# A four-block cross-attention network with routed experts: roots, routing pieces and weight loads of block 4

## The chip, the cores and the metric

The program runs on one core of a Trainium2 chip. Its time is the device time of one execution in microseconds (us); several executions are made and the median counts. All data are float32. The names of the engines are those of the profile: PE is the matrix engine, PEld its weight loads, DVE the vector engine, ACT the scalar engine, POOL GpSimd, SP the engine that issues most DMA transfers.

## What is computed

There are 16 sequences of 128 tokens with 256 features. Four blocks follow one another, each a cross-attention to a context and a feed-forward part, both behind a gate:

```python
x = x + tanh(g_xattn[i]) * xattn_i(layernorm(x), ctx)
x = x + tanh(g_ffn[i])   * ffn_i(layernorm(x))
```

Blocks 2 to 4 have routed experts in their feed-forward part (8 with 2 chosen, 16 with 4 chosen, 64 with 8 chosen). The change is mostly in block 4. Its attention has 16 heads of 16 features. Queries and keys are layer-normalised head by head, and the keys are of two kinds, each with a softmax of its own whose results are added:

```python
kv_dca = (y_dca @ Wkv_dca + bkv_dca)          # last 16 context tokens
k_dca, v_dca = ln(kv_dca[..., 0], ...), kv_dca[..., 1]
q = ln(x @ Wq + bq)                           # per head, eps 1e-6
k, v = ln(y_main @ Wk + bk), y_main @ Wv + bv # first 112 context tokens
ctx = attn(q, k, v) + attn(q, k_dca, v_dca)
return ctx @ Wo + bo
```

and its feed-forward part has 64 experts of width 96 and room for 128 tokens each:

```python
probs = softmax(x @ router_weight.T)
topw, topi = top_k(probs, 8);  topw = topw / topw.sum()
pos = position of the token among those of the same expert, in order
xe[topi, pos] = x                              # dropped where pos >= 128
h = silu(xe @ gate) * (xe @ up);  ye = h @ down
y = sum over the 8 chosen of topw * ye[topi, pos]
```

## The kernel before

**What stays where.** All of x lies in SBUF (`x_sb`, 128 tokens by 16 sequences by 256 features) for the whole program. Weights and context come by DMA; the rows for the experts go through two DRAM tensors per block, `xs_f` (rows sent to the experts) and `y_f` (the experts' results, by token and choice).

**Routing** (class `Routed`, lines 100 to 290) of a block's feed-forward part runs inside the attention before it. When the attention has added its result to x for the second sequence of a pair, `done` queues that pair's pieces, and each `tick` of the attention's loop runs the ones that are due: `stats`, `rows` (normalised rows into `hx`), `turn` (transposes), `logits`, `top` (the eight largest), `first` (the chosen experts as a mask and the weights), `places` (prefix sums as matmuls), `targets` (rows `hrow` in `xs_f`), then the sends. In block 4 there are four send pieces per pair, each with four indirect DMAs that POOL issues (L240), so 8 for each of the 16 sequences, 128 in all. A send is kept in order after the latest per-head normalisation on POOL (`mark`). What is left over runs in `finish`, at the start of the feed-forward part.

**Results of block 3's experts** are added to x late: `settle` fetches a sequence's four results of 128 x 256 (`fetch`, a DMA of 512 KB by SP into one of two buffers) and adds them with four dependent DVE instructions (`add`, L287). In block 4's attention the settles and the layer normalisation of x are placed by `norm_steps(sp, -3, 4)` in groups of four sequences: group 0 ahead of the loop, and for the groups 1 to 3 the settles eight to five iterations before they are needed, but never before iteration 0.

**Block 4's attention** (`xattn3`, from line 1250) is a loop over `b` in 0 to 17. In iteration `b` it works on several sequences at once. PE, DVE and ACT run in the order in which the loop is written (`manual_schedule`, L1441); POOL and SP are ordered by the scheduler. In the order of the loop:

- `normalise_qk(b+2)`: sums of squares per head (L1322), then the inverse root on DVE (`inverse_root`, L392: an integer guess and three Newton steps, twelve small instructions with the scaling), then two multiplications on POOL (L1327).
- `scores(b)` (32 small matmuls into four PSUM banks), and `maxima(b, ...)` of bank 0 (L1376), which are written beside the queries so that the next product subtracts them.
- `add_up(b-1)` (sums of exponentials, and their reciprocals `rd`, L1413) and `values(b-1)`, then the maxima of banks 1 to 3.
- `project(b-2)`: the output product (L1436), a further matmul that adds the bias (L1437), and the addition to x (L415).
- `quotients(b-1)`: `rd` spread over the heads (L1425), copied by ACT, multiplied into `aT` (L1430).
- `tick(b-2)`.
- `with_maxima(b)` (queries turned again), `project_qk(b+3)`, `exponentials(b)` (32 matmuls, then four ACT exponentials, L1389), `project_v(b)`, `squares(b+3)` and `turn_qk(b+2)`.
- the normalisation steps of this iteration, and a second `tick`.

The layer normalisation of x takes its inverse root from POOL (`power`, L390). PSUM is shared out as four banks `sc`, two `tr`, one `av` and one `pj`.

**The experts of block 4** (`ffn3`). A loop over steps `n`, with SP and PE in written order: `load(n)` (gate and up weights `wgu`, 192 KB in one of five buffers, and the expert's 128 rows `xe`, 140 KB in one of four), `load_down(n-1)` (`wdn`, 96 KB, five buffers), `up(n-3)`, `turn(n-2)`, `down(n-4)`. `turn` transposes `xe` (L795), and `destination` (L262 to L269) works out on DVE the row in `y_f` to which each result goes (`drow`, six buffers). `down` ends with an indirect DMA by POOL (L273). Every `xe` has to wait for all sends of the routing.

**Store.** For each sequence the eight results are fetched (1024 KB, four buffers), added by eight DVE instructions, and x is written out.

Of the kernel before, what the change touches and what calls it, by code (L numbers as in the profile page):

```python
# [91 lines left out]
class Routed:  # L92
# [24 lines left out]
    def done(self, b):  # L117

        if b % 2 == 1:
            for i, f in enumerate(self.pieces(b // 2)):  # L120
                self.due.setdefault(self.now + 1 + i, []).append(f)

    def tick(self):
        self.now += 1
        for f in self.due.pop(self.now, ()):
            f()

    def finish(self):
        self.net.mark = None
        for n in sorted(self.due):  # L130
            for f in self.due[n]:
                f()
        self.due = {}

    def pieces(self, p):
        net, nc, sp, E, K = self.net, self.net.nc, self.sp, self.E, self.K
        b0 = 2 * p
# [6 lines left out]
        def stats():  # L144
            h["stats"] = net.ln_stats(sp, b0, 2)

        def rows():
            x = tile("x", [P, 2, self.W], bufs=4)
            net.ln_rows(sp, b0, h["stats"], 2, to=x)

        def turn():
            net.ln_turn(b0, [h["x"][:, j, 0:D] for j in range(2)])

        def logits():
            lg = net.psum("tr", [P, 2, E])
            for j in range(2):
# [4 lines left out]
            mx = tile("mx", [P, 2])  # L161
            nc.vector.tensor_reduce(mx, lg, AX.X, ALU.max)
            sh = tile("sh", [P, 2, E])
            nc.vector.tensor_tensor(sh, lg, mx.unsqueeze(2).to_broadcast([P, 2, E]), ALU.subtract)
# [3 lines left out]
        def top():  # L168
            top, idx, x = tile("top", [P, 2, 8]), tile("idx", [P, 2, 8], U32), h["x"]
            for j in range(2):  # L170
                nc.vector.max(top[:, j, :], h["sh"][:, j, :])
                nc.vector.max_index(idx[:, j, :], top[:, j, :], h["sh"][:, j, :])
            nc.vector.tensor_copy(x[:, :, D : D + K], idx[:, :, 0:K])
            nc.vector.tensor_copy(x[:, :, D + K : D + 2 * K], self.ids[:, b0 : b0 + 2, :])
            w = tile("w", [P, 2, K])
            nc.scalar.activation(w, top[:, :, 0:K], AF.Exp)
            if self.over_all:
                nc.scalar.activation(tile("ex", [P, 2, E]), h["sh"], AF.Exp)

        def chosen():  # L180

            m, x = tile("m", [P, 2, E]), h["x"]
            if K == 8:
                for j in range(2):
                    nc.vector.match_replace(m[:, j, :], h["top"][:, j, :], h["sh"][:, j, :], 1.0)
                nc.vector.tensor_scalar(m, m, 0.5, None, ALU.is_gt)
            else:
                iota = net.cst[:, C_IOTA : C_IOTA + E].unsqueeze(1).to_broadcast([P, 2, E])
                for k in range(K):
                    dst = m if k == 0 else tile("m1", [P, 2, E])  # L190
                    nc.vector.tensor_tensor(dst, x[:, :, D + k : D + k + 1].to_broadcast([P, 2, E]), iota, ALU.is_equal)
                    if k:
                        nc.vector.tensor_tensor(m, m, dst, ALU.add)
            for j in range(2):
# [4 lines left out]
        def weights():  # L199
            den = tile("den", [P, 2])  # L200
            nc.vector.tensor_reduce(den, h["ex"] if self.over_all else h["w"], AX.X, ALU.add)
            nc.vector.reciprocal(den, den)
            nc.vector.tensor_scalar(den, den, self.gate, None, ALU.mult)
            nc.vector.tensor_tensor(
                h["x"][:, :, D + 2 * K :], h["w"], den.unsqueeze(2).to_broadcast([P, 2, K]), ALU.mult
            )

        def places():
            pos = net.psum("tr", [P, 2, E])
# [4 lines left out]
                pf, net.ones, self.before[:, b0 : b0 + 2, :].rearrange("p b e -> p (b e)"), start=False, stop=True  # L214
# [3 lines left out]
        def targets():  # L218
# [4 lines left out]
            enc = tile("enc", [P, 2, E])  # L223
            base = net.cst[:, self.base : self.base + 2 * E].rearrange("p (b e) -> p b e", b=2)
            nc.vector.tensor_tensor(enc, pos, base, ALU.add)
            nc.vector.tensor_tensor(enc, enc, m, ALU.mult)
            r8 = tile("r8", [P, 2, 8])
            for j in range(2):
                nc.vector.max(r8[:, j, :], enc[:, j, :])
            row = tile("row", [P, 2, K], U32, bufs=4)  # L230
            if self.spare:
                own = tile("own", [P, 2, K])
                nc.vector.tensor_scalar(own, self.ids[:, b0 : b0 + 2, :], float(-self.tiles * P), None, ALU.add)
# [15 lines left out]
        sends = [partial(send, j, range(k, k + many)) for j in range(2) for k in range(0, K, many)]  # L249

        def first():
            chosen()
            weights()
# [30 lines left out]
    def add(self, b, yg):  # L284
        x = self.net.x[:, b, :]
        for k in range(self.K):
            self.net.nc.vector.tensor_tensor(x, x, yg[:, k, :], ALU.add)  # L287


class Net:  # L290
    def __init__(self, tc, ctx, t, out):
# [17 lines left out]
        self.head = self.routed = None  # L309

# [81 lines left out]
    def inverse_root(self, v, n):  # L392
# [3 lines left out]
        half = self.sb(self.small, "half", [P, n], I32)  # L396
        nc.vector.tensor_scalar(half, v.bitcast(I32), 1, None, ALU.logical_shift_right)
        guess = self.sb(self.small, "guess", [P, n], I32)
        nc.vector.tensor_scalar(guess, half, -1.0, float(0x5F3759DF), ALU.mult, ALU.add)
        y = guess.bitcast(F32)  # L400
        for _ in range(3):
            t = self.sb(self.small, "nt", [P, n])
            nc.vector.tensor_tensor(t, y, y, ALU.mult)
# [1263 lines left out]
```

## Time and profile before

| what | us |
|---|---|
| runs | 2452.39, 3353.52, 2457.0 |
| median | 2457.0 |
| profiled execution | 2455.75 |
| its span | 2453.8 |
| mean granted clock of PE | 0.924 |

By the shares of the page PE is busy for 81% of the span, DVE for 60%, ACT for 36%, POOL for 33%. The stages follow one another with little overlap. Their borders, read from the timeline:

| stage | from, us | to, us |
|---|---|---|
| block 1 | 0 | 485 |
| block 2, attention and experts | 485 | 950 |
| block 3, attention | 950 | 1510 |
| block 3, experts | 1510 | 1822 |
| block 4, entry of the attention (weights, constants, first normalisations) | 1822 | 1860 |
| block 4, attention loop | 1860 | 2174 |
| block 4, only routed rows are sent | 2174 | 2232 |
| block 4, 64 experts | 2232 | 2385 |
| last additions and output | 2385 | 2454 |

A timeline line shows the start, the duration, engine, source line, operation, the tiles written and read with their shapes, how many instructions stand together, and in square brackets the engine's idle time before them with what ended it. In the waits, each line gives engine and waiting operation, what it waited for, then the total, the number of waits and the longest.

### The profile page before, as it was taken

To read this page: it belongs to the slowest core of one execution; us is meant where nothing else is said; L and a number is where in the kernel's file an instruction comes from. 1 tells how busy PE (TensorE), PEld (TensorE's weight loads), DVE (VectorE), ACT (ScalarE), POOL (GpSimd) and SP (SyncE) were. 2 spreads that over 40 slices of the span, in tenths; PEclk is the share of its full clock that TensorE was granted. 3 is DMA by queue.
4 is the path that set the end of the run, shared out by engine and by line. 5 is a ranking of instruction groups with operands and counts; after the bars stand their busy time and mean duration, and the time that the engine had idled before them with its cause. 6 is when DMAs were issued, how large, how long until landed. Compare 5 with 4: busy or idle time off the path is not lost. (4 is left out here: it accounts for less than half of the span.)

```text
span 2453.8 us, 38199 instructions
## 1 busy us (share of the span) xinstructions
PE 1998.5 (81%) x12988; PEld 1404.4 (57%) x12988; DVE 1483.7 (60%) x4176; ACT 879.1 (36%) x1868; POOL 806.2 (33%) x799
## 2 busy tenths in 40 slices
PE   8999998788887786999898997899965878744760
PEld 5776675356665553666565665566644766633550
DVE  4676765378986444666667665455556676432438
ACT  3433333266663123444443443122212434211320
POOL 1121111143544222334444444222230035564440
PEclk9999998899998899999999999999986899767995
DMA  5159951109201772000000001578752001226768
GB/s 178 69 134 270 303 154 35 52 2 343 94 19 55 230 245 76 18 1 25 21 21 21 16 17 67 182 245 250 247 194 69 19 27 67 74 93 194 243 220 291
DMA packets 198529, 299.32 MB, mean 122 GB/s; under 512 B 21514, under 2 KB 151025, under 8 KB 195905
## 3 DMA queue, kind: packets, MB, share of 16 engines
q1 hardware_dynamic: 175776, 238.90, 32.7%
q0 software_dynamic: 19488, 55.31, 6.1%
q10 hardware_dynamic: 3072, 2.68, 0.3%
q8 instruction: 105, 1.72, 0.3%
q14 instruction: 88, 0.71, 0.1%
HBM read 160.92 MB, written 135.90 MB: 121 GB/s over the span
## 5 line engine op out<-in xcount | busy, mean ns | idle before, releaser
L548 POOL TENSOR_TENSOR e<-e,r 128x512 f32<-128x512 f32 x128 | 132.7, 1037 | 565.7 <-DVE r L547 284.9
L273 POOL DMA_INDIRECT y_f<-ys,drow x182 | 174.5, 959 | 394.7 <-DVE ys L1076 212.0
L240 POOL DMA_INDIRECT xs_f<-hx,hrow x224 | 221.5, 989 | 105.9 <-issue 56.5
L536 ACT ACTIVATE e<-e 128x512 f32<-128x512 f32 x128 | 80.7, 630 | 476.2 <-DVE e L533 476.2
L1054 PE MATMUL mm<-wgu,xeT 128*128 128x352 f32 x472 | 166.9, 477 | 8.8 <-DVE xeT L1047 6.6
L1163 PE MATMUL qk<-wa,xnT 128*128 128x512 f32 x256 | 127.3, 620 | 24.0 <-DVE nq L1177 23.9
L543 DVE TENSOR_REDUCE sm<-e 128x4 f32<-128x512 f32 x128 | 87.8, 686 | 93.1 <-ACT e L536 93.1
L795 PE MATMUL tr<-cst,xe 128*128 128x128 f32 x364 | 72.3, 281 | 77.8 <-DMA xe<-xs_f 77.4
L1074 PE MATMUL o<-wdn,hT 88*128 88x256 f32 x472 | 122.0, 381 | 2.0 <-ACT hT L1067 2.0
L667 PE MATMUL y<-wb,aT 128*128 128x256 f32 x512 | 121.2, 380 | 1.0 <-DVE x_sb L415 1.0
L667 PEld LDWEIGHTS y<-wb,aT 128*128 128x128 f32 x512 | 97.3, 190 | 41.6 <-issue 18.2
L1216 PE MATMUL y<-wb,aT 128*128 128x256 f32 x512 | 121.0, 380 | 0.0
L633 PE MATMUL mm<-xnT,wm 128*128 128x512 f32 x256 | 120.1, 594 | 0.0
L795 PEld LDWEIGHTS tr<-cst,xe 128*128 128x128 f32 x364 | 46.3, 144 | 123.4 <-issue 85.3
L390 POOL TENSOR_TENSOR rr<-ss,nhalf 128x8 f32<-128x8 f32 x64 | 105.9, 1655 | 29.4 <-DVE ss L1171 29.3
L287 DVE TENSOR_TENSOR x_sb<-x_sb,yg 128x256 f32<-128x256 f32 x224 | 93.4, 423 | 32.0 <-DMA yg<-y_f 26.1
L1177 DVE TENSOR_TENSOR nq<-qk,rr 128x512 f32<-128x512 f32 x64 | 44.2, 691 | 113.1 <-POOL rr L390 113.1
L1067 ACT COPY hT<-tr 88x256 f32<-88x256 f32 x118 | 43.4, 368 | 181.5 <-PE tr L1065 181.3
L873 DVE TENSOR_REDUCE mx<-sc 128x4 f32<-128x512 f32 x128 | 84.6, 681 | 37.7 <-PE sc L866 37.7
L1054 PEld LDWEIGHTS mm<-wgu,xeT 128*128 128x128 f32 x472 | 81.7, 193 | 43.3 <-DVE xeT L1047 14.7
L521 PEld LDWEIGHTS tr<-cst,e 128*128 128x128 f32 x512 | 63.4, 141 | 69.9 <-issue 60.8
L1216 PEld LDWEIGHTS y<-wb,aT 128*128 128x128 f32 x512 | 92.7, 191 | 11.3 <-issue 1.2
(287 smaller groups left out, 4777.5 us busy)
## 6 DMA issues: line engine op xcount, KB each, us to landing
wgu<-in_L_W SPq DMA_DIRECT2D x118, 352.0 KB
xs_f<-zeros SPq DMA_DIRECT2D x32, 1072.0 KB
wdn<-in_L_W SPq DMA_DIRECT2D x118, 176.0 KB
xs_f<-zeros SPq DMA_DIRECT2D x16, 1048.0 KB
y_f<-zeros SPq DMA_DIRECT2D x16, 1024.0 KB
yg<-y_f SPq DMA_DIRECT2D x16, 1024.0 KB
wgu<-in_L_gu SPq DMA_DIRECT2D x64, 192.0 KB
xe<-xs_f SPq DMA_DIRECT2D x79, 134.0 KB
```

The costliest lines, as they stand in the source:

```text
L240: ins = nc.gpsimd.indirect_dma_start(out=self.rows, out_offset=bass.IndirectOffsetOnAxis(ap=h["row"][:, j, k : k + 1], axis=0), in_=h["x"] ...
L273: self.net.unordered("y_" + self.name, self.net.nc.gpsimd.indirect_dma_start(out=self.y, out_offset=bass.IndirectOffsetOnAxis(ap=row, axis ...
L287: self.net.nc.vector.tensor_tensor(x, x, yg[:, k, :], ALU.add)
L390: return self.nc.gpsimd.tensor_tensor(out, var, self.nhalf[:, :n], ALU.pow)
L548: nc.gpsimd.tensor_tensor(e, e, r.unsqueeze(2).to_broadcast([P, 4, S]), ALU.mult)
L633: nc.tensor.matmul(mm, wm[:, kk, 4 * hq + j, :], self.xnT[:, kk, g * 512 : (g + 1) * 512], start=kk == 0, stop=kk == 1,)
L667: nc.tensor.matmul(y, a[:, j, :], wn[:, 4 * hq + j, :], start=j == 0, stop=j == 3)
L795: self.nc.tensor.transpose(tr[:, kk, :], src[:, kk * P : (kk + 1) * P], self.ident)
L1054: nc.tensor.matmul(gu, xeT[:, kk, :], wgu[:, kk, :], start=kk == 0, stop=kk == 1)
L1074: nc.tensor.matmul(y, hT[:, c, :], wdn[:, c, :], start=c == 0, stop=c == 1)
L1163: nc.tensor.matmul(q, self.xt(kk, b), wq[:, kk, cols], start=kk == 0, stop=kk == 1)
L1216: nc.tensor.matmul(y[b], a[:, j, :], wn[:, h, :], start=h == 0, stop=h == 15)
```

## The change

- **Inverse roots in block 4.** `inverse_root` becomes an ACT logarithm, an ACT exponential and one Newton step of three DVE instructions. It is split in two: `deviations(b)` (sums, logarithm, exponential) and `normalise_qk(b)` (Newton step, multiplications). The layer normalisation of x and of the routing in block 4 uses it too, in place of `power`. One table of ACT functions that holds both is loaded ahead of the loop.
- **Interleaving.** Pieces and norm steps are generators; `weave` takes one instruction from each in turn, so that dependent small DVE instructions of several stand alternately. All blocks use it.
- **Order in block 4's loop.** All maxima stand directly behind the scores, a `tick` behind them, and only then `add_up`, `values` and the rest. There are three ticks per iteration in place of two, and five once no new sequence is left.
- **Layer normalisation by pairs.** `norm_pairs` spreads settles and statistics over odd and even iterations; two settles stand ahead of the loop.
- **The output bias** is added to x by POOL, after the normalised rows have been taken (`add_bias`), in place of the matmul. `add_up` writes to bank `pj` in place of `tr`.
- **Routing.** The sequences 14 and 15 are routed one at a time, the others in pairs.
- **Experts.** Both weights of an expert are loaded 14 steps ahead of its rows, in 18 buffers each.

```diff
@@ Routed
     def done(self, b):
-        if b % 2 == 1:
-            for i, f in enumerate(self.pieces(b // 2)):
+        alone = self.K == 8 and b >= B - 2
+        if alone or b % 2 == 1:
+            for i, f in enumerate(self.pieces(b, 1) if alone else self.pieces(b - 1, 2)):
                 self.due.setdefault(self.now + 1 + i, []).append(f)
...
+def weave(fs):
+    left = [g for g in [f() for f in fs] if g is not None]
+    while left:
+        left = [g for g in left if next(g, left) is not left]
@@ Net
-    def inverse_root(self, v, n):
+    def inverse_root(self, v, n, scale, eps):
         nc = self.nc
-        half = self.sb(self.small, "half", [P, n], I32)
-        nc.vector.tensor_scalar(half, v.bitcast(I32), 1, None, ALU.logical_shift_right)
...
-        for _ in range(3):
...
+        y = self.sb(self.small, "guess", [P, n])
+        nc.scalar.activation(y, v, AF.Ln, scale=scale, bias=eps[0])
+        nc.scalar.activation(y, y, AF.Exp, scale=-0.5)
+        yield y
+        t = self.sb(self.small, "nt", [P, n])
+        nc.vector.scalar_tensor_tensor(t, v, eps[1] / scale, y, ALU.add, ALU.mult)
+        nc.vector.scalar_tensor_tensor(t, t, -0.5 * scale, y, ALU.mult, ALU.mult)
+        z = self.sb(self.small, "ny", [P, n])
+        nc.vector.scalar_tensor_tensor(z, t, 1.5, y, ALU.add, ALU.mult)
+        yield z
@@ ln_stats
+        if self.eps is not None:
+            root = self.inverse_root(mv[:, :, 1], n, 1.0, (self.eps, LN_EPS))
+            next(root)
+            yield
+            return mv, next(root)
@@ xattn3
+            def add_bias(b0):
+                for b in (b0, b0 + 1):
+                    nc.gpsimd.tensor_tensor(self.x[:, b, :], self.x[:, b, :], byrow, ALU.add)
...
             def add_up(b):
-                sm = self.psum("tr", [P, S])
+                sm = self.psum("pj", [P, S])
...
-                    nc.tensor.matmul(y, a[:, c, :], wo4[:, c, :], start=c == 0, stop=False)
-                nc.tensor.matmul(y, self.ones[0:1, :], bo, start=False, stop=True)
+                    nc.tensor.matmul(y, a[:, c, :], wo4[:, c, :], start=c == 0, stop=c == 3)
...
+            def norm_pairs():
...
+                for p in range(2, B // 2):
+                    s, held = 2 * p - 3, {}
+                    for i, f in enumerate((
+                        partial(self.settle, sp, 2 * p, int(p > 2)), partial(self.settle, sp, 2 * p + 1, int(p > 2)),
+                        partial(stats, p, held), partial(rows, p, held), partial(turned_rows, p, held),
+                    )):
+                        steps.setdefault(divmod(max(0, 2 * (s - 2) + i), 2), []).append(f)
...
+                nc.scalar.preload_act_table_set("natural_log_exp_and_others")
+                self.eps = lneps
...
+                weave([partial(self.settle, sp, 4, 2)])
+                norm = norm_pairs()
                 for b in range(B + 2):
-                    if b + 2 < B:
-                        normalise_qk(b + 2)
                     if now:
                         banks = scores(b)
-                        maxima(b, banks, (0,))
+                        maxima(b, banks, range(4))
+                    self.tick()
                     if back:
                         add_up(b - 1)
                         values(b - 1)
                     if now:
-                        maxima(b, banks, (1, 2, 3))
+                        with_maxima(b)
+                    if b + 2 < B:
+                        deviations(b + 2)
+                    if back:
+                        quotients(b - 1)
+                    if now:
+                        exponentials(b)
+                    if b + 2 < B:
+                        normalise_qk(b + 2)
+                    self.tick(None, norm.get((b, 0), ()))
+                    if not now:
+                        self.tick()
                     if late:
                         project(b - 2)
-                    if back:
-                        quotients(b - 1)
-                    self.tick(b - 2 if late else None)
...
+                    self.tick(b - 2 if late else None, norm.get((b, 1), ()))
                     if b + 3 < B:
                         project_qk(b + 3)
-                    if now:
-                        exponentials(b)
-                        project_v(b)
-                    if b + 3 < B:
                         squares(b + 3)
                     if b + 2 < B:
                         turn_qk(b + 2)
+                    if now:
+                        project_v(b)
+                    if not now:
+                        self.tick()
@@ ffn3
-            def load(e, _):
-                wgu = self.sb(sp, "wgu", [P, 2, 2 * F], bufs=5)
+            def weights(e, _):
+                wgu = self.sb(sp, "wgu", [P, 2, 2 * F], bufs=AHEAD + 4)
                 nc.sync.dma_start(wgu, t["L3_gu"][e])
+                wdn = self.sb(sp, "wdn", [F, D], bufs=AHEAD + 4)
+                nc.sync.dma_start(wdn, t["L3_dn"][e])
+                return wgu, wdn
+
+            def load(e, held):
+                wgu, wdn = held
                 xe = self.sb(sp, "xe", [P, r.W], bufs=4)
...
-            def load_down(e, held):
-                wdn = self.sb(sp, "wdn", [F, D], bufs=5)
-                nc.sync.dma_start(wdn, t["L3_dn"][e])
-                return (*held, wdn)
...
-            steps = ((load, 0), (load_down, 1), (up, 3), (turn, 2), (down, 4))
+            steps = ((weights, 0), (load, AHEAD), (up, AHEAD + 3), (turn, AHEAD + 2), (down, AHEAD + 4))
```

## The prediction

> **What bounds the kernel now.** First the busy time by stage, one answer over windows set at the stage borders (columns: window, length, then busy us and instructions of PE, PEld, DVE, ACT, POOL, then granted clock, DMA share, GB/s). Only the stages from 1860 us on are touched by more than the order of small DVE instructions.
>
> ```profile
> core 0: us, PE busy (x) PEld busy (x) DVE busy (x) ACT busy (x) POOL busy (x), PEclk, DMA share, GB/s
> 1860.00:1908.00 48.00, 25.42 (x258) 20.45 (x254) 31.11 (x91) 12.31 (x23) 3.59 (x6) 0.61 0.26 88
> 1908.00:2160.00 252.00, 205.94 (x2448) 167.58 (x2442) 157.41 (x569) 90.63 (x179) 98.78 (x113) 0.87 0.14 51
> 2174.00:2232.00 58.00, 5.07 (x20) 3.91 (x20) 9.86 (x58) 1.02 (x3) 44.37 (x47) 0.53 0.33 117
> 2232.00:2385.00 153.00, 114.22 (x768) 89.55 (x768) 68.72 (x320) 49.02 (x129) 60.24 (x64) 0.97 0.77 237
> 2385.00:2454.00 69.00, 0.00 (x0) 0.00 (x0) 53.15 (x128) 0.02 (x1) 1.26 (x2) 0.51 0.77 278
> ```
>
> These are the first two iterations of block 4's attention, the other iterations, a hole in which only POOL works, 64 experts, and the last additions with the stores. In the first window PE is half idle at a clock of 0.61. The timeline of DVE there, then of PE:
>
> ```profile
> 1868.48 3.50 DVE L287 TENSOR_TENSOR x_sb<-x_sb,yg 128x256 f32<-128x256 f32 x8
> 1873.68 1.80 DVE L287 TENSOR_TENSOR x_sb<-x_sb,yg 128x256 f32<-128x256 f32 x4 [1.69 <-DMA yg<-y_f]
> 1876.25 1.80 DVE L287 TENSOR_TENSOR x_sb<-x_sb,yg 128x256 f32<-128x256 f32 x4 [0.77 <-DMA yg<-y_f]
> ...
> 1883.52 3.51 DVE L287 TENSOR_TENSOR x_sb<-x_sb,yg 128x256 f32<-128x256 f32 x8
> ...
> 1891.51 1.80 DVE L287 TENSOR_TENSOR x_sb<-x_sb,yg 128x256 f32<-128x256 f32 x4 [0.83 <-DMA yg<-y_f]
> ```
>
> ```profile
> 1898.27 2.05 PE L1425 MATMUL tr<-rd,wd 128*128 128x128 f32 x8 [8.26 <-DVE rd L1413]
> ```
>
> Block 3's expert results are added to eight sequences at the end of iteration 0, in two groups of four; they stand ahead of iteration 1's maxima and of rd, so PE waits 8.26 us for rd. In the hole:
>
> ```profile
> 2170.84 1.04 POOL L240 DMA_INDIRECT xs_f<-hx,hrow  x1 [11.41 <-DVE hrow L234]
> 2172.19 0.96 POOL L240 DMA_INDIRECT xs_f<-hx,hrow  x1 [0.30 <-issue]
> ...
> 2231.17 0.97 POOL L240 DMA_INDIRECT xs_f<-hx,hrow  x1 [0.30 <-issue]
> ```
>
> Those are the last 48 sends of routed rows, back to back at (2232.1−2170.8)/48 = 1.27 us; every expert's load must follow them. Among the experts, the waits from 2220 to 2370 and two lines of SP and DVE:
>
> ```profile
> DVE drow L269 <- DMA y_f<-ys,drow: 47.3, 44, 2.2
> ```
>
> ```profile
> 2251.58 0.37 SPq L1496 DMA_DIRECT2D xe<-xs_f  x1
> ```
>
> ```profile
> 2254.76 0.18 DVE L262 SCALAR_TENSOR_TENSOR eq<-xe 128x16 f32<-128x16 f32 x1 [0.36 <-DMA xe<-xs_f]
> ```
>
> DVE runs ahead and waits 44 times for a buffer of drow, held by a result still on its way out; a loaded xe takes 3.2 us from issue to use. An expert takes 2.28 us (first turns of experts 3 and 63: 2244.05 and 2381.09), the fastest ones 1.87.
>
> **The change, part by part.**
>
> *Blocks 1 to 3.* Block 1 is as before. In 2 and 3 only the order of small DVE instructions within a routing piece changes. One such step in the trace takes 0.22 us start to start, so a dozen overlapped latencies per pair are worth 1 or 2 us, against a PE that is 91% busy in block 3: 2.
>
> *Early hole.* Scores(0), (1) and (2) started at 1859.5, 1884.3 and 1907.6. After, only the two settles of sequences 4 and 5 stay ahead of the loop, the others come two per odd iteration up to the ninth. Chained by hand with the durations of later iterations, the first two take 12 and 14 us instead of 24.8 and 23.3: 48.1 − 26 = 22 gained, less 1 for a longer entry (normalisation in two halves, one more matmul, a table load that moves ahead): 21. The fetches of 512 KB move with them on SP, which has nothing else in this stage.
>
> *Iterations 2 to 15*, 252.8 us before (scores(2) at 1907.6 to add_up(15) at 2160.4), 18.1 each. Removed per iteration: nine of twelve small DVE steps of the root (2.0 us), the bias matmul L1437 (0.69 on PE), POOL's pow (0.72 and 1.06 us in its rows). That pow matters where it queues behind sends: in 1908–2160 `hx` waited on it 15.8 us in 3 waits, one of 12.4. Added: Ln and Exp on ACT, for which no row exists; nearest is ACT's Exp of 128x16 at 0.22, with 0.60 (128x512) as the other end, so 0.45 for the two, 0.4 to 1.2; it lies beside ACT's 90 busy of 252. Two DVE steps wait for it, behind them quotients' multiply and, on POOL, the normalise, whose user is turn_qk half an iteration later. POOL adds the bias, two instructions of about 0.62 per pair (row of the 128x256 multiply), behind up to 12 sends (15 us); the next normalise queues behind both with 4 to 6 us to spare, so nothing, and up to 8 per hit if the spare is gone.
>
> The new order makes this chain in an even iteration: scores 1.2, eight maxima 2.75, the routing piece now behind them 1.4, rd 0.95 = 6.3; then PE's quotients 1.16, exponentials 1.17, project 2.0, project_qk 2.2, turns 1.04, project_v 1.3 = 8.9; pieces' and normalisation's matmuls 1.8 and hand-overs 1.0: 18.0. Before, rd came after the first of four maxima, so PE now waits some 2.7 us for it. An odd iteration with two settles of 1.8 is DVE-bound: of the 3.6 some 2.0 lie beside PE: 19.6. Without settles and normalisation 16.3. Sum: 4 × 19.6 + 4 × 18.0 + 3 × 16.3 + 15.6 + 13.8 + 12.6 = 241: 11 gained.
>
> [...] Granted clock is 0.61 and 0.87 in the first two windows and 0.53 in the hole. [...]
>
> *Sends.* At add_up(15), pairs 5, 6 and 7 had nothing sent; the end came 71.7 us later. After, pair 5's targets come one iteration sooner, but pair 4's last sends hold POOL until about 4.3 us past add_up(15); 48 × 1.27 = 60.7 follow: 65, so 6.7 gained. Routing sequences 14 and 15 singly costs about six more instructions per step (2 us of DVE, idle there) and has them ready some 25 us past add_up(15), when POOL is free only at 45: nothing, and without that backlog up to 8 either way.
>
> *Experts.* 15 × 288 KB of weights go into the hole (4.3 MB at the 237 GB/s of the expert window is 18 us): hidden. By the instruction order SP now issues in step n: wgu(n), wdn(n), xe(n−14). wdn(n) takes the buffer of wdn(n−18), read by PE's last matmul of that very step. So xe queues behind that wait, where it went off a step earlier; its use is the turn two steps on. Hence period ≥ (1.4 + L)/2, with 1.4 from the down's end over the two issues of 0.4 and the turn's place in its step, and L from issue to use. The row: L = 3.2 loaded, 2.03 alone (2233.62 to 2235.65). With 96 KB ahead of it on the queue in place of 192, 2.8: 2.1 for 45 experts, and 1.87 to 1.9 for the last 14, whose weights are in. Saving 45 × 0.18 + 14 × 0.38 = 13; at 3.2, 5. [...] The drow wait goes, since eq no longer runs two experts ahead.
>
> *Store:* unchanged.
>
> Sum: 2 + 21 + 11 + 7 + 12 = 53. The profiled execution took 2455.75 us (span 2453.8), 1.3 below the median of 2457.0: 2455.75 − 53 is about **2402**.
>
> **The rivals.**
> *More of PE's waits go* (0.19): the spread pieces fit beside PE and an iteration averages 15.6, near PE's 14.7 busy; 14 × 1.6 = 23 more: 2379. For it: DVE has 157 of 252 us busy. Against: maxima, piece and rd are one chain.
> *Middle iterations gain nothing* (0.10): spread settles and clock give the 11 back and some 10 more, half of the experts' gain goes: about 2430.
> *The experts get slower* (0.15), the other side: xe behind wdn's wait, as above, with landings that lengthen as every transfer of the loop is asked for at the same moment. It decides, as slower than before, from L = 5.1 (period 3.2, 45 × 0.92 = 41, what the rest gains). At L = 6 the period is 3.7 and 64 are lost: 2479; at 7.5 it is 4.45, 98 lost: 2513, which I give for it. For it: the DMA share is already 0.77, and with one step of lead nothing else can hide a late load. Against: the longest landing seen was 3.9.
> *It does not do what it says:* Ln and Exp might alternate tables at 1.28 us a load (row of L1389), but the order holds one load in this attention.
>
> **How the numbers follow.** The main sum has 0.56, with 15 us around it. 2% is about what a measurement of this kernel can tell from no change: below 2408, above 2506. About 0.64 of the main case and all of the first rival are faster: 0.36 + 0.19 = 0.55. The rest of the main case and the second rival make 0.30. The slower rival spreads from 2457 to 2540, with two thirds of it over 2506: 0.10 slower, and 0.35 the same. The range leaves out 0.06 of the first rival and nearly all of the slower one: 2372 to 2456.
>
> **Signs.** One table load in the attention; scores(2) near 1887; even and odd iterations near 18 and 19.6 with PE's quotients waiting for rd; last send near 2190; drow's waits gone, SP's wdn waiting for PE, 2.1 us per expert and 1.9 for the last 14. I am wrong if iterations are above 19 on average, if normalise waits behind sends, or if xe takes over 4 us to its use.

## The result, and the profile after

The changed kernel took 2417.16 us (median of four runs, 2409.52 to 2419.63) beside 2454.8 us for the kernel before: a ratio of 0.984, with an interval from 0.982 to 0.986. That is 1.6% faster. One of the four runs of the kernel before, at 3353.52 us, is a slow one and does not count in the ratio. The forecast was 2402 with a range from 2372 to 2456. The profiled execution took 2419.28 us, its span is 2416.3.

The two traces were cut at the same events: the first scores of sequences 0 and 2, the sums of exponentials of sequence 15 (`add_up(15)`), the end of the last send, the start of the last expert's transposes, and the end.

| stretch | before, us | after, us | difference | forecast |
|---|---|---|---|---|
| start to scores(0) | 1859.5 | 1853.7 | −5.8 | −1 |
| scores(0) to scores(2) | 48.1 | 27.0 | −21.2 | −22 |
| scores(2) to add_up(15), 14 iterations | 252.7 | 249.2 | −3.6 | −11 |
| add_up(15) to last send | 71.8 | 62.9 | −8.9 | −7 |
| last send to the last transposes | 149.0 | 151.7 | +2.7 | −12 |
| last transposes to the end | 72.7 | 72.0 | −0.7 | 0 |

The sum is −37.5, which is the difference of the spans. The first row is mostly scatter: in four further kernels of the first group of runs below, whose program is the same up to there, scores(0) began between 1851.6 and 1862.2. So the gain is the early hole and the sends, close to the forecast's sizes; the long middle of the attention gave a third of what was expected, and the experts gave nothing. The busy time of the same stages, again with window, length, busy us of PE, PEld, DVE, ACT, POOL, then clock, DMA share and GB/s:

```profile
1853.70:1880.60 26.90, 20.03 (x253) 16.08 (x252) 17.39 (x47) 13.05 (x29) 4.13 (x6) 0.87 0.19 62
1880.60:1946.00 65.40, 51.54 (x697) 41.72 (x696) 43.52 (x136) 31.84 (x71) 8.03 (x12) 0.97 0.12 41
1946.00:2048.00 102.00, 78.44 (x897) 64.99 (x896) 62.51 (x211) 39.33 (x87) 45.29 (x52) 0.85 0.18 63
2048.00:2130.00 82.00, 63.67 (x848) 52.63 (x852) 46.18 (x172) 34.24 (x74) 46.15 (x51) 0.90 0.21 78
```

The first row is the early stretch: PE is busy for 20 of 27 us at a clock of 0.87, where it was busy for 25 of 48 at 0.61. The second row, iterations 2 to 5, runs at 0.97. In the third, iterations 6 to 10, into which more of the routing and its sends falls (POOL is busy for 45 us, where it was for 8), the clock is 0.85. One iteration there, on PE (iteration 8):

```profile
1989.32 1.06 PE L1460 MATMUL av<-e,vx 128*32 128x128 f32 x32
1991.32 0.66 PE L1389 MATMUL tr<-cst,qk 128*128 128x128 f32 x4 [0.94 <-DVE qk L1429]
1994.22 1.51 PE L1478 MATMUL tr<-rd,wd 128*128 128x128 f32 x8 [2.25 <-DVE rd L1466]
1995.66 2.09 PE L1417 MATMUL sc<-qT,kT 18*128 18x128 f32 x32
1997.69 1.11 PE L494 MATMUL tr<-cst,hx 128*128 128x128 f32 x4
1998.59 3.43 PE L1489 MATMUL pj<-wb,aT 128*128 128x256 f32 x8
```

PE waits 0.94 us for the maxima and 2.25 us for rd, with 0.66 us of work between; the products behind that gap then take 2.09 us in place of 1.17, and the output product 3.43 in place of 2.0. The gap costs some 2.3 us more after it has ended. The granted clock of that stretch, cut where it changes (columns as above):

```profile
1988.10:1994.90 6.80, 3.61 (x90) 2.98 (x83) 6.09 (x19) 0.93 (x2) 0.00 (x0) 1.00 0.01 2
1994.90:2001.70 6.80, 6.80 (x49) 5.72 (x48) 2.67 (x11) 3.92 (x10) 3.16 (x4) 0.50 0.07 24
2001.70:2015.40 13.70, 10.70 (x170) 9.00 (x168) 8.94 (x26) 5.07 (x11) 11.04 (x12) 1.00 0.31 105
```

The clock is full until the gap has ended and half for 6.8 us behind it. In both first traces only these two values occur, and in the 14 iterations the half clock comes in stretches of 3.4 us or a multiple of that: 51 us in all here, 65 us in the kernel before. Each of the five pairs of waits of about 0.9 and 2.25 us is followed within 1.4 us by 6.8 us at half. So 0.85 is a mean of full and half. The waits of PE over all 14 iterations (1880 to 2130):

```profile
PE tr L1478 <- DVE rd L1466: 20.8, 14, 2.2
PE tr L1389 <- ACT qT L1395: 11.3, 5, 2.9
PE pj L1360 <- DVE x_sb L438: 8.3, 7, 2.0
```

The first is one per iteration, as expected; the second was in no sum. It lies in odd iterations: `squares` stands ahead of `turn_qk` on ACT and waits for an addition that DVE makes only after the settles, and PE waits for the copy qT behind it. The waits of `squares` in the same window:

```profile
ACT sq L1368 <- DVE qk L1364: 36.7, 12, 5.8
```

Among the experts, the waits of DVE (2185 to 2340) and of SP (2150 to 2340), and a piece of the chain of waits (start, length, what):

```profile
DVE eq L279 <- DMA xe<-xs_f: 91.7, 48, 36.9
DVE drow L286 <- DMA y_f<-ys,drow: 7.8, 9, 1.5
```

```profile
SPq L1586 <- PE o L1620: 45.1, 43, 4.2
```

```profile
2218.60 4.14 DMA xe<-xs_f
2222.87 0.41 PE tr L834 x2
2223.28 0.45 PE o L1620 x2
2224.17 3.33 DMA xe<-xs_f
```

drow's waits have nearly gone (47.3 us before), and SP's wdn waits 43 times for PE's `down`, as read from the order. The chain shows the loop: a down lets SP go on, SP asks for an xe, the xe lands 3.3 to 4.1 us later, and its transposes are followed by the next down. Matching the 64 issues with the 64 uses gives 3.27 us from issue to use for experts 4 to 49, and 2.39 us per expert, where 2.8 and 2.1 had been taken.

POOL's sends behind add_up(15), which began at 2129.8:

```profile
2132.27 0.96 POOL L258 DMA_INDIRECT xs_f<-hx,hrow  x1 [5.48 <-DVE hrow L252]
```

The sends of the pairs 0 to 4 were over at 2126.8. POOL then waits 5.48 us for the rows of pair 5, and from 2132.3 on the last 48 sends follow without a gap.

### The profile page after: what moved, and what is told of

Same layout as the page of the kernel before. It is cut to its first block, busy times and chain, and to the rows that moved or that the text cites. A ratio compares the mean times of both kernels' runs of the same rounds, so it can differ in the third digit from the quotient of the medians.

```text
span 2416.3 us, 38004 instructions
## 1 busy us (share of the span) xinstructions
PE 1988.6 (82%) x12962; PEld 1390.9 (58%) x12962; DVE 1456.3 (60%) x4083; ACT 897.0 (37%) x1932; POOL 809.5 (33%) x807
## 5 line engine op out<-in xcount | busy, mean ns | idle before, releaser
L304 DVE TENSOR_TENSOR x_sb<-x_sb,yg 128x256 f32<-128x256 f32 x224 | 94.6, 429 | 23.1 <-DMA yg<-y_f 11.3
L1254 PEld LDWEIGHTS y<-wb,aT 128*128 128x128 f32 x512 | 92.6, 190 | 11.4 <-issue 1.2
```

What stands on the lines that cost most here:

```text
L1254: nc.tensor.matmul(y[b], a[:, j, :], wn[:, h, :], start=h == 0, stop=h == 15)
```

## The experiments

The kernels ran in three groups. In the first group the kernel before took 2452 us, in the second and third 2505 and 2508. Times are therefore compared through the ratio to the kernel before of the same group. The changed kernel itself was run again in the third group only; it is the yardstick for the second too, which assumes that these two groups are alike. In stage times below, the 14 iterations are counted on DVE, from the first maximum of sequence 2 to the reciprocal rd of sequence 15 (250.1 us in the changed kernel's first trace; some expectations give up to 2.5 us less for this stretch). The experts' stage goes from the last send to the last transposes. In the eight kernels that have the changed experts' loop as it is, it took 149.8 to 154.0 us, without a difference between the groups; each kernel has one trace.

**Rows ahead of weights.**

```diff
-            steps = ((weights, 0), (load, AHEAD), (up, AHEAD + 3), ...
+            steps = ((load, AHEAD), (weights, 0), (up, AHEAD + 3), ...
```

> The changed kernel with one line altered: in each step of the experts' loop the rows xe are asked for ahead of the two weights, so that xe no longer stands behind wdn's wait for PE in the same step but behind that of the step before. Theory A (the order of SP's queue: one step of lead, period = (1.4 us + landing)/2 = 2.34 with the landing of 3.27 us measured in the changed kernel): with two steps of lead the queue no longer binds, the period of experts 4 to 49 falls from 2.39 to about 1.95, the stage from the last send to the last expert's transposes from 152 to 132 us, the whole from 2417 to about 2397. Rival B (the transfers themselves are the limit, DMA share 0.69 to 0.77 in this stage): landing grows as they are asked for sooner, the period stays above 2.3 and the time within 4 us of 2417.

Measured: 2411.69 us, ratio 0.982 (0.979 to 0.985); the experts' stage 148.3 us, 2.33 us per expert. Theory A falls: a step more of lead in the order of SP bought 3 us of 20, which puts the stage just below the range of the unaltered loop, and the ratio's interval overlaps the changed kernel's (0.982 to 0.986). From issue to use an xe now takes 3.59 us, longer, as B says. A small part of that is seen at SP itself:

```profile
2241.58 0.33 SPq L1586 DMA_DIRECT2D wdn<-in_L_dn  x1
2242.00 2.03 SPq L1593 DMA_DIRECT2D xe<-xs_f  x1
```

The issue of this xe takes 2.03 us. Three of the 64 take more than 1 us; the median is 0.39.

**The experts' loop of before**, in the changed kernel (`weights` and `load` replaced by the old `load` and `load_down`).

> The changed kernel with the experts' loop of the kernel before (weights five buffers deep, asked for beside their rows); the attention is the changed one. Theory A: loading 14 experts ahead has given nothing so far, since its gain is lost to xe's place in SP's queue; the stage from the last send to the last transposes goes from 152 back to about 149 us, the whole to about 2414. Rival B (weights loaded in the hole do relieve the transfers): the stage gets 10 us or more longer than 149, the whole above 2427.

Measured: 2414.27 us, ratio 0.985 (0.983 to 0.988); the stage is 147.8 us, 2.29 per expert. The loads 14 experts ahead are worth nothing that this run can show: the stage is 4 us shorter without them, 2 below the range of the loop with them, and the two ratios' intervals overlap. B, which had it 10 us longer, falls.

**Squares behind the turns.**

```diff
                     if b + 3 < B:
                         project_qk(b + 3)
-                        squares(b + 3)
                     if b + 2 < B:
                         turn_qk(b + 2)
+                    if b + 3 < B:
+                        squares(b + 3)
```

> The changed kernel with one pair of statements exchanged: squares(b+3) stands behind turn_qk(b+2) in ACT's order, not ahead of it. Theory A: in odd iterations the settles on DVE delay the addition that makes qk, squares waits for it on ACT, and the copy qT of turn_qk, which needs nothing of it, is queued behind: PE waited 11.3 us in 5 waits (longest 2.9) for qT at L1389. The waits go and the 14 iterations from scores(2) to add_up(15) shorten from 249 to about 239 us. Rival B: the addition itself delays the next steps (project_v shares the one bank pj), and PE waits there instead: within 3 us of 249.

Measured: 2407.5 us, ratio 0.982 (0.980 to 0.985); the 14 iterations took 238.2 us, but the first two 2.5 us more. The same waits, from 1884 to 2120:

```profile
PE tr L1389 <- DVE qk L1429: 7.3, 13, 0.9
PE tr L1389 <- ACT qT L1395: 6.5, 5, 2.5
```

Of the 11.3 us of waits for qT 6.5 are left. The three kernels with the unaltered loop (the two above and the changed kernel) took 250.4, 245.3 and 250.1 us, on average 248.6 with a scatter of 5. So the loop won 10 us, as theory A says, but the wait is only halved, and what else shortened the loop was not tried. The interval of the whole time overlaps the changed kernel's.

**The routing piece behind rd.**

```diff
-                    self.tick()
                     if back:
                         add_up(b - 1)
                         values(b - 1)
                     if now:
                         with_maxima(b)
+                    self.tick()
```

> The changed kernel with the first tick of an iteration moved behind add_up, values and the second turning of the queries, so that the reciprocal rd stands ahead of the routing piece on DVE. Theory A: PE's waits for rd (20.8 us in 14 waits, longest 2.2) stem from the piece that stands between the maxima and rd; they fall to some 6 us, and with fewer idle gaps PE's granted clock rises over 0.90: the 14 iterations go from 249 to about 232 us. Rival B: the pieces only move on and delay the root's sums and aT on DVE: within 4 us of 249.

Measured: 2403.56 us, ratio 0.980 (0.977 to 0.982), which lies below the changed kernel's interval; the 14 iterations took 231.0 us. PE's wait for rd (1891 to 2120), and the windows over iterations 2 to 5, 6 to 10 and 11 to 15:

```profile
PE tr L1478 <- DVE rd L1466: 1.8, 9, 0.2
```

```profile
1889.00:1954.00 65.00, 51.02 (x697) 41.20 (x696) 43.51 (x136) 31.49 (x70) 8.03 (x12) 0.99 0.12 41
1954.00:2048.00 94.00, 74.55 (x927) 60.08 (x925) 60.51 (x212) 39.71 (x91) 45.61 (x51) 0.92 0.19 68
2048.00:2121.00 73.00, 58.98 (x839) 47.67 (x843) 44.77 (x171) 32.04 (x71) 44.99 (x50) 0.95 0.23 83
```

Theory A. The clock went from 0.85 and 0.90 to 0.92 and 0.95 over the same iterations; the time at half clock fell from 51 to 24 us. The wait for rd fell by 19 us; against the mean of 248.6 for the three unaltered loops the iterations gained 18. That the clock's gain does not come on top has its reason in other waits, which grew: for x_sb from 8.3 to 11.4 us, for qT ahead of L1478 from none to 4.3. Over the three windows PE is busy for 184.6 us, where it was for 193.7, and idle for 47.4, where it was for 55.7: some 9 us come from faster products, and only 8 of the 19 from less idle time. The tail from rd to the last send gave 3 us back (63.7 us for 60.8): the sends of pair 5 began 2.9 us later after rd.

**Most weights left out.**

```diff
             def weights(e, _):
+                if e >= AHEAD + 4:
+                    return kept[e % (AHEAD + 4)]
...
+                kept.append((wgu, wdn))
...
-            steps = ((weights, 0), (load, AHEAD), (up, AHEAD + 3), ...
+            steps = ((load, AHEAD), (weights, 0), (up, AHEAD + 3), ...
```

The experts 18 to 63 use the weights of the first 18 again, so this kernel leaves out their loads. It and the next have the rows ahead of the weights.

> The kernel with rows xe ahead of the weights, and in addition only the first 18 experts load weights of their own; experts 18 to 63 use those again (the weight loads of 46 experts are left out, 13.6 MB of traffic and the waits of wdn for PE). Theory B (the loaded transfers set the pace: an xe takes 3.3 to 3.6 us from issue to use, 2.0 to 2.1 when nothing else is under way): landing goes to about 2.5 us and the period of experts 18 to 63 from 2.3 to 1.9, the fastest ones' pace; the stage from the last send to the last transposes from 148 to about 131 us. Rival C (the chain of PE, ACT, DVE and POOL's send of the result sets 2.3): the stage stays above 143 us.

**Weights asked for by ACT.**

```diff
-                nc.sync.dma_start(wgu, t["L3_gu"][e])
+                nc.scalar.dma_start(wgu, t["L3_gu"][e])
...
-                nc.sync.dma_start(wdn, t["L3_dn"][e])
+                nc.scalar.dma_start(wdn, t["L3_dn"][e])
...
-            steps = ((weights, 0), (load, AHEAD), (up, AHEAD + 3), ...
+            steps = ((load, AHEAD), (weights, 0), (up, AHEAD + 3), ...
```

> The kernel with rows xe ahead of the weights, and in addition the experts' weights are asked for by ACT instead of SP, so that xe is alone in SP's queue; the traffic is the same. Theory B1 (xe lands late because it stands behind 288 KB of weights in the same queue): landing falls from 3.6 to about 2.5 us and the stage from 148 to about 135 us. Theory B2 (xe shares the 16 engines' bandwidth with everything that is under way, whichever queue asks): landing stays above 3.2 us, the stage within 4 us of 148; two more issues of 0.4 us per expert on ACT cost nothing, ACT being busy for 47 of 152 us.

Measured: 2463.11 us (0.983, 0.980 to 0.985) without the weights, 2467.93 us (0.984, 0.981 to 0.986) with them on ACT's queue; the changed kernel in the third group has 0.989 (0.987 to 0.992). The stage is 136.6 us without the loads and 140.9 us with them on the other queue. So of the 11.7 us between 148.3 (first group) and 136.6, some 7 come back when xe no longer shares SP with the weights, and some 4 only when the traffic itself is gone. The stage lies between what B1 and B2 expect (135 and 148), so neither is the whole. No issue of an xe takes more than 0.43 us in these two. With weights on ACT, SP runs ahead, the landing can no longer be read from issue to use, and another wait is back (2235 to 2370):

```profile
DVE drow L286 <- DMA y_f<-ys,drow: 33.0, 38, 1.4
```

**Settles bunched again.**

```diff
-                        partial(self.settle, sp, 2 * p, int(p > 2)), partial(self.settle, sp, 2 * p + 1, int(p > 2)),
+                        partial(self.settle, sp, 2 * p, 6 if p == 3 else int(p > 5)), partial(self.settle, sp, 2 * p + 1, int(p > 5)),
...
-                        steps.setdefault(divmod(max(0, 2 * (s - 2) + i), 2), []).append(f)
+                        steps.setdefault((0, 1) if i == 0 and p == 3 else divmod(max(0, 2 * (s - 2) + i), 2), []).append(f)
```

> The changed kernel with the settles of the sequences 6 to 11 put back into iteration 0, as in the kernel before (only the places of the additions and fetches change). Theory A: the first two iterations go from 27 back to about 45 us, since these 24 additions and their fetches stand ahead of iteration 1's maxima; the 14 iterations after them gain at most 6 us from having three odd iterations without settles (248 to 242). Whole: 2417 to about 2429. Rival B: the spread additions cost as much later as they save at first; the 14 iterations fall by 15 us or more and the whole stays within 4 us.

Measured: 2488.59 us, ratio 0.993 (0.991 to 0.996) beside the yardstick's 0.989 (0.987 to 0.992). From the first maximum of sequence 0 to that of sequence 2 it takes 45.8 us, the yardstick 28.8; the 14 iterations 291.3 and 299.6. So 17 lost and 8 won: theory A, with 2 us more won later than it allowed.

**Roots as before.** (The Newton steps of before in `inverse_root`, and `self.eps = lneps` taken out, so that POOL's pow returns.)

> The changed kernel with the inverse roots as before: twelve small instructions on DVE for the heads' roots (at the place of the three Newton instructions) and POOL's pow for the layer normalisation's. Theory A (the prediction's): nine DVE instructions of 0.22 us, 2.0 us per iteration, return to a chain that is partly bound by DVE, and pow waits behind sends on POOL: the 14 iterations go from 248 to about 262 us. Rival B: the root lies beside PE's exponentials and has slack; the gain came from the order alone: within 4 us of 248.

Measured: 2497.79 us, ratio 0.997 (0.995 to 0.998) beside the yardstick's 0.989: some 14 to 18 us slower. The 14 iterations took 317.1 us, 17 more than the yardstick's 299.6, and the first two 2 more. Theory A. The heads' roots and the layer normalisation's were put back together, so their shares are not known. Together they are worth about two thirds of what the whole change brings beside the yardstick (1.1%).

**The changed kernel again, the last sequences as a pair, and the combinations.**

> The changed kernel once more, unaltered, as the yardstick for the other three on the same chip: a ratio to the kernel before of 0.984, or up to 0.990 if this chip grants PE a lower clock in the attention's later iterations, as the one of the second group of runs did.

> The changed kernel with the last two sequences routed as a pair again. Theory A (the prediction's): POOL's backlog of 48 sends of 1.27 us covers the later readiness, the stage from the last reciprocal rd to the last send stays within 2 us of 61 and the whole within 4 us of the changed kernel. Rival B: the pair's sends come late enough to leave POOL idle; the stage gets 4 to 8 us longer.

```diff
-        alone = self.K == 8 and b >= B - 2
+        alone = False
```

> The changed kernel with both orders that shortened the loop when tried alone: squares behind turn_qk, and the first tick behind the second turning of the queries. Alone they took the stretch of iterations 2 to 15 from 243 to 249 us down to 236 and 230. Theory A (they remove different waits of PE, for qT and for rd): both together reach 218 to 224 us, the whole 22 to 28 us below the changed kernel. Rival B (what they save overlaps): not below 228.

> The kernel with both orders of the loop, and in the experts' loop rows ahead of weights, weights asked for by ACT, and twelve buffers in place of six for the result rows drow and weights dw in block 4. With weights on ACT's queue the experts' stage was 141 us and DVE waited 38 times, 33 us in all, for a buffer of drow. Theory A: those waits go and PE's own pace of 1.9 to 2.0 us per expert is reached, the stage is 130 us; the whole lies 45 us below the changed kernel. Rival B (the waits for drow hide behind PE): the stage stays at 141 us, the whole 33 to 36 us below.

| kernel | us | ratio, interval | 14 iterations | rd(15) to last send | experts |
|---|---|---|---|---|---|
| changed kernel again | 2483.52 | 0.989 (0.987 to 0.992) | 299.6 | 65.7 | 152.1 |
| last two as a pair | 2477.48 | 0.988 (0.986 to 0.989) | 298.8 | 67.2 | 152.5 |
| both orders | 2463.56 | 0.982 (0.981 to 0.984) | 278.7 | 72.5 | 152.5 |
| both orders, weights on ACT, 12 buffers | 2457.12 | 0.982 (0.978 to 0.985) | 278.0 | 68.5 | 140.2 |

The pair: its stage is 1.5 us longer and the intervals overlap, so routing the last two singly is worth nothing that these runs can show. That is theory A's number, but not its reason. When POOL has made the sends of sequences 10 to 13, it waits for the rows of sequence 14, in the changed kernel and with the pair (the first line names the DVE instruction that was last seen; hrow itself is written from 2236.95 on):

```profile
2237.40 0.96 POOL L258 DMA_INDIRECT xs_f<-hx,hrow  x1 [5.36 <-DVE nt L428]
2232.82 0.95 POOL L258 DMA_INDIRECT xs_f<-hx,hrow  x1 [6.75 <-DVE hrow L252]
```

So in this group no backlog covers the late rows. They are ready 47.5 us past add_up(15) in the first line's trace, 21.6 us in the changed kernel's first trace, which has no such gap.

Both orders: 21 us less in the iterations and 20 in the whole, where theory A had 22 to 28. In the tail 7 us are given back (72.5 for 65.7 us): its sends begin 3.2 us after rd in place of 0.4, and POOL idles 9.4 us for rows in place of 5.4. Whether the two orders add up stays open, since each alone had won 18 and 10 in the first group.

Twelve buffers: the waits for drow are gone, but the stage stays at 140 us, as B says, and DVE waits for xe in 41 places instead (2215 to 2345, the first wait being for the sends):

```profile
DVE eq L279 <- DMA xe<-xs_f: 55.9, 41, 17.2
```

Both combinations are faster than the changed kernel of the same group, by 0.7 to 0.8% by their ratios. The second lies 26 us below it, less than both theories had for the whole (45, and 33 to 36).

## Why the forecast came out as it did

The time lies in the forecast's range, but above 2408 us. A time within 2% of the kernel before had been given 0.35, a faster one 0.55. Of the 53 us 37.5 came.

**The early hole.** Right in mechanism and size: 21.2 measured, 22 forecast. The bunched settles show that these are the main cause: 17 us come back with six of them.

**Sends.** Right in size: 8.9 measured, 6.7 forecast. The path to it was another, so the closeness is in part luck. The forecast had pair 4's last sends hold POOL until 4.3 us past add_up(15). They were over 3.0 us before it, and POOL waited for the rows of pair 5, as it did in the kernel before. These rows now come earlier: the last 48 sends begin 2.4 us past add_up(15) in place of 10.5. They follow at 1.26 us each, and in this trace they do cover the single routing, as forecast.

**Iterations 2 to 15.** The direction was right, the size wrong: 3.6 measured, 11 forecast. (With the two other kernels of the first group that have the same loop, it is 3 to 8 against the one trace of before.) The whole stretch, before and after, in the columns of the windows above:

```profile
1907.63:2160.36 252.73, 206.67 (x2449) 167.95 (x2448) 158.13 (x571) 91.36 (x180) 98.97 (x113) 0.87 0.14 51
1880.65:2129.82 249.17, 193.43 (x2430) 159.16 (x2429) 152.07 (x518) 105.37 (x229) 99.47 (x114) 0.90 0.18 62
```

PE's busy time fell by 13 us, but its idle time rose by 10, from 46.1 to 55.7. Two terms failed.

First, the wait for qT in odd iterations (11.3 us) was left out. It comes from `squares` on ACT, queued behind a DVE addition that the settles delay. The forecast put 2.0 of each 3.6 us of settles beside PE and didn't ask what ACT had queued behind that addition. With `squares` behind the turns this wait is nearly halved and the loop 10 us shorter.

Second, the wait for rd was foreseen (2.7 us per iteration, 1.5 measured), but the clock behind it was priced at nothing: the sum takes the 11 whole. That such a wait costs only its own length was the author's estimate, and no run shows it. The trace shows a cost: behind waits of 0.94 and 2.25 us close together the clock is at half for 6.8 us, and two products take nearly double (2.09 us in place of 1.17, 3.43 in place of 2.0). With the piece moved behind rd the loop won 18 us, half of it from faster products.

The mean clock of the stretch still rose, from 0.87 to 0.90. What was right: the roots. Put back, they cost 17 us in the 14 iterations. The interleaving, the bias on POOL and the other bank for `add_up` were not put back singly, so their shares are not known.

**Experts.** The queueing was read rightly from the order: SP's wdn waits 43 times for `down`, xe behind it, and (1.4 + 3.27)/2 = 2.34 is close to the 2.39 measured. What failed is the landing: 2.8 was taken because less would stand ahead of xe in the queue, against a loaded row of 3.2. It was 3.27. With the row itself the same sum gave a gain of 5. The 12 in the forecast's sum, chosen near the 13 of that landing, is shown by no run: the stage got 2.7 us longer. The forecast also set 2.28 against every expert, which is the mean over all: the experts 4 to 49 took 2.33 before and the last 14 took 2.16. Against these the middle lost 2.4 us and the last 14, at 2.05 and not 1.9, won 1.5; the first four lost 1.7. Together that is about the 2.7 measured. And the queueing is not the only limit: with that wait a step further off, the period only went from 2.39 to 2.33. Taking the weights off SP's queue brings it to 2.18. What keeps it there, where the last 14 experts of the best kernel run at 1.91, is not settled beyond DVE's waits for xe.

**The rivals.** The slower one needed a landing above 5.1 us; the longest in the changed kernel was 4.2. That the middle gains nothing, with half of the experts' gain gone, was about as near as the main sum: 13 us above the time measured, where the main sum lies 15 below. One table load in block 4's attention, as read (1.28 us, ahead of the loop).

## What to carry to other kernels

Before a piece is moved to a place where it hides, see what stands behind it on its own engine and who waits for that: here a routing piece between maxima and a reciprocal cost the wait and, with PE's clock at half for 6.8 us, in the iteration shown some 2.3 us more in the products behind it. Removing one wait gains less than the wait when others grow behind it: of 19 us only 8 came off PE's idle time. Ask whether loads are late before loading them far ahead; here the transfer that ended the wait was another one in the same queue, and loading ahead brought nothing (the stage took 151.7 us with it, 147.8 without). When an estimate needs a landing time under load, take the loaded row, not a better one argued from what will stand ahead of it (here 3.2 us was the row, 2.8 was taken, 3.27 came).

## What the runs showed of the hardware

The change is worth 1.6% in the first comparison and 1.1% in the third group, where the kernel before took 2508 us and the changed one 2483.52. The attention's 14 iterations take 299.6 us there in place of 250.1, with the blocks ahead of it within 9 us. From 1882 to 1945 PE's mean clock is 0.97 in both traces; from 1945 to 2140 it is 0.77 there, where the first trace has 0.87 from 1945 to 2130. The first and the third group of experiments carry the chip number 3, the second carries 1, so the number does not tell them apart. The waits of PE's weight loads and of its matmuls in the changed kernel of the third group (1945 to 2140):

```profile
PEld pj L1460 <- issue: 27.5, 38, 1.3
```

```profile
PE pj L1460 <- issue: 15.3, 25, 1.7
```

In the changed kernel's first trace neither line occurs from 1945 to 2140. The stalls are in `add_up`, 64 small weight loads and matmuls in a row with `values`, in iterations in which POOL is sending rows (7 sends from 2028 to 2040); PE waits for nothing that the trace names. All eight kernels of the second and third group show them in this loop's `add_up` or `values`; in those of the first they are below 0.5 us. This trace also holds fewer updates of semaphores (from which the profile infers what released an engine) than instructions that make one: for PE's semaphore 2176 of 2334, where the first has 2334 of 2334. So some of its waits can carry a wrong name or none. What PE lacks there was not tried, and the cause stays open.
